# Scatter rows of a mixture-of-experts block: made on GpSimd between two scatters, two blocks ahead, as a sum in place of a maximum

## The chip, the cores and the metric

The kernel runs on one core of a Trainium2 chip. The metric is the device time of one execution in microseconds; before the change the median of three runs is 561.6 us (561.57 to 562.12). A core has a matrix engine (TensorE, PE in the profile), VectorE (DVE), ScalarE (ACT), GpSimd (POOL) and SyncE (SP), which only issues transfers. Each engine runs its own instructions in order, and they wait for one another through semaphores. Transfers (DMAs) are issued by SyncE, ScalarE and GpSimd; the scatters here are issued by GpSimd[...].

## What is computed

One transformer layer on 8 sequences of 512 tokens with 128 features, all in float32:

```
x = layernorm(x + attention(x))          # 16 heads, causal
probs = softmax(x @ gate_w.T)            # 14 experts
top2_p, top2_i = top_k(probs, 2)
w = top2_p / max(top2_p.sum(-1), 1e-10)
hh = gelu(x @ w1[e] + b1[e])             # 128 -> 256, for each expert e
all_out = hh @ w2[e] + b2[e]             # 256 -> 128
moe_out = w[:, 0] * all_out[top2_i[:, 0]] + w[:, 1] * all_out[top2_i[:, 1]]
x = layernorm(x + clip(x + moe_out, -100, 100))
```

Each token goes to the two experts with the highest probabilities, so there are 2 x 4096 = 8192 pairs of a token and an expert.

## The kernel before

The attention part works through the sequences in an order written out by hand (`jobs`, `at`). For each sequence `route` picks the two experts of every token, and GpSimd scatters the tokens' rows into a buffer `XS` in HBM, sorted by expert (`scatter("XS", ...)`, L793). A row has 130 numbers: 128 features, the weight of this expert (column `D`), and the row of the output buffer `OS` that the result belongs to (column `D + 1`, a whole number in float32).

The expert part then goes over `NBLK` = 45 blocks of `BT` = 256 rows of `XS`, each of one expert. The first `EARLY` = 11 blocks are full ones, planned from the first six sequences. The other 34 can have rows behind an expert's last token; for these `beyond` is 1,000,000 in the rows that hold no token and 0 in the others, so that their target lies outside `OS` and the scatter leaves them out (`bounds_check` = 8191). An iteration of the loop over the blocks (L1142) gives out, in this order:

- `load(i + 4)`: SyncE loads the block's rows into `xb`, one of six buffers (`into`).
- `begin(i + 2)`: ScalarE copies the expert's weights (`weights`), and `turn` has TensorE transpose the rows (L1048) and VectorE copy them out of PSUM into `xT` (L1050, named `bxT` in the profile). `turn` also makes the block's target rows on VectorE: for late blocks the maximum of column `D + 1` and `beyond` (L1054, `bto`), and for all blocks the cast to int32 (L1058, `bto_i`).
- `expert_in(i + 1)`: the first matmuls (L1066, `h`) and ScalarE's gelu (L1071, `hT`).
- `expert_out(i)`: the second matmuls (L1082, `o`); then for each half `s` of 128 rows VectorE multiplies by the weight (L1090, `ob`, eight buffers), and GpSimd scatters the half into `OS` by `bto_i` (L233).
- after every fourth block from block 12 on, `biases` of one sequence: a transpose (L1101, `wp`), a copy on VectorE (L1107, `wT`), a matmul (L1109, `bp`), and an addition on VectorE (L1112).

The routing of the last sequence (`last_route`, with its eight scatters into `XS`) and the plan of the late blocks are given out in pieces among the first blocks; dummy rows behind every expert's last token are written by SyncE and ScalarE (`fill`, L804 and L807). The first late block's load waits for all scatters into `XS`. When all scatters into `OS` have landed, the tail gathers the two results of each token, adds them and normalises.

Of the kernel before, what the change touches and what calls it, by code (L numbers as in the profile page):

```python
# [10 lines left out]
ALU = mybir.AluOpType  # L11
# [25 lines left out]
def kernel(  # L37
# [18 lines left out]
    nc = tc.nc  # L56
    B, T, D = x.shape
    E, _, F = w1.shape
# [9 lines left out]
    NBLK = (2 * N + E * (BT - 1)) // BT  # L68


    EARLY = -(-(2 * (B - 2) * T - E * (BT - 1)) // BT)
# [160 lines left out]
    def scatter(key, dst, idx, src, bound):  # L232
        inst = nc.gpsimd.indirect_dma_start(  # L233
            dst,
            bass.IndirectOffsetOnAxis(ap=idx, axis=0),
            src,
            None,
            bounds_check=bound,
            oob_is_err=False,
        )  # L240
        tc.declare_no_dep(inst.ins, group=key, reason="no two of them write the same row")
        tc.add_to_no_dep_group(key, inst.ins)
        scatters.setdefault(key, []).append(inst.ins)
        return inst
# [18 lines left out]
    with tc.tile_pool(name="work", bufs=2) as work, tc.tile_pool(  # L263
# [9 lines left out]
        def bank(name, dt=FP):  # L273
            return ps_m.tile([P, 2048 // mybir.dt.size(dt)], dt, tag="bank", name=name)
# [4 lines left out]
        wt = bank("wt")  # L279
# [317 lines left out]
        def divide(u):  # L597
            b, g = divmod(u, NG)
            oT = outs.pop(u)
            tr = bank(f"tr_{u}")  # L600
            for qb in range(NQ):
                nc.tensor.transpose(
                    tr[:, qb * P : (qb + 1) * P], oT[:, qb * P : (qb + 1) * P], ident
                )
            tr_v = tr.rearrange("p (q j s) -> p q j s", j=GH, s=HS)
            rec = work.tile([P, NQ, GH, 1], FP, tag="rec", name=f"rec_{u}")
            nc.vector.reciprocal(rec, tr_v[:, :, :, HD : HD + 1])
            if g == 0:
                attns[b] = work.tile(
                    [P, NQ, NG, GH, HD], FP, tag="attn", name=f"attn_{b}", bufs=1  # L610
                )
            nc.vector.tensor_tensor(
                attns[b][:, :, g],
                tr_v[:, :, :, 0:HD],
                rec.to_broadcast([P, NQ, GH, HD]),
                ALU.mult,
            )

        def project(b):

            attn = attns.pop(b)
            tp = bank(f"at_{b}")
            for qb in range(NQ):
                nc.tensor.transpose(
                    tp[:, qb * P : (qb + 1) * P],
                    attn[:, qb].rearrange("p g j d -> p (g j d)"),
                    ident,
                )
            aT = work.tile([P, T], FP, tag="aT", name=f"aT_{b}", bufs=1)
            nc.scalar.copy(aT, tp)  # L630
            outs["a", b] = aT, outs.pop(("x", b))
# [261 lines left out]
        beyond = plan.tile([P, SB, P], FP, tag="beyond", name="beyond")  # L893
# [85 lines left out]
                    at(r + 2, statistics, b, (2, 3))  # L979
                    at(r + 3, proceed, r + 3, route(b), 1)  # L980

        blocks = {}

        def load(i):
            where = wheres[i >= EARLY]
# [28 lines left out]
        s = -2  # L1014
# [20 lines left out]
        def weights(i):  # L1035
            n = i if i < EARLY else i - EARLY
            at_w = nc.scalar.value_load(
                wheres[i >= EARLY][0:1, 1, n : n + 1], min_val=0, max_val=(E - 1) * WW
            )
            wt = ffn.tile([P, WW], FP, tag="wt", name=f"wt_{i}", bufs=4)  # L1040
            nc.scalar.copy(wt, WR[:, bass.ds(at_w, WW)])  # L1041
            blocks[i].insert(1, wt)

        def turn(i):
            xb = blocks[i][0]
            tp = ps_x.tile([P, BT], FP, tag="x", name=f"x_{i}")
            for s in range(SB):
                nc.tensor.transpose(tp[:, s * P : (s + 1) * P], xb[:, s, 0:D], ident)  # L1048
            xT = ffn.tile([P, BT], FP, tag="xT", name=f"bxT_{i}")
            nc.vector.tensor_copy(xT, tp)  # L1050
            to = xb[:, :, D + 1]
            if i >= EARLY:
                to = ffn.tile([P, SB], FP, tag="to", name=f"bto_{i}")
                nc.vector.tensor_tensor(  # L1054
                    to, xb[:, :, D + 1], beyond[:, :, i - EARLY], ALU.max
                )
            to_i = ffn.tile([P, SB], I32, tag="to_i", name=f"bto_i_{i}", bufs=NBLK)
            nc.vector.tensor_copy(to_i, to)  # L1058
            blocks[i] += [xT, to_i]

        def expert_in(i):
            xb, wt, xT, to_i = blocks[i]
            hp = ps_h.tile([P, NFC, BT], FP, tag="h", name=f"h_{i}")
            hT = ffn.tile([P, NFC, BT], FP, tag="hT", name=f"hT_{i}")
            for f in range(NFC):
                nc.tensor.matmul(  # L1066
                    hp[:, f, :], wt[:, f * P : (f + 1) * P], xT, start=True, stop=True
                )
            for f in range(NFC):
                c = F + NFC * D + f  # L1070
                nc.scalar.activation(  # L1071
                    hT[:, f, :], hp[:, f, :], AF.Gelu, bias=wt[:, c : c + 1]
                )
            blocks[i].append(hT)

        def expert_out(i):
            xb, wt, xT, to_i, hT = blocks.pop(i)
            op = ps_o.tile([P, SB, D], FP, tag="o", name=f"o_{i}")
            ob = ffn.tile([P, SB, D], FP, tag="ob", name=f"ob_{i}", bufs=8)
            for s in range(SB):  # L1080
                for f in range(NFC):
                    nc.tensor.matmul(  # L1082
                        op[:, s, :],
                        hT[:, f, s * P : (s + 1) * P],
                        wt[:, F + f * D : F + (f + 1) * D],
                        start=(f == 0),
                        stop=(f == NFC - 1),
                    )
            for s in range(SB):
                nc.vector.tensor_scalar(  # L1090
                    ob[:, s, :], op[:, s, :], xb[:, s, D : D + 1], 0.0, ALU.mult, ALU.add
                )
                scatter("OS", OS[:, :], to_i[:, s : s + 1], ob[:, s, :], 2 * N - 1)


        acc = z_sb = x_sb
# [22 lines left out]
        def begin(i):  # L1119
            weights(i)  # L1120
            turn(i)
# [11 lines left out]
                fill(place_i, e)  # L1133

        begin(0)
        divide(u)
        begin(1)
        project(b)
        expert_in(0)
        residual(b)  # L1140
        statistics(b, range(NQ))
        for i in range(NBLK):  # L1142
            if i + AHEAD < NBLK:
                load(i + AHEAD)
            if i < 3:
                go_on(1)
            if i == 3:
                place_i = fill_place()
                late = plan_late()
                fills(range(0, 4))  # L1150
                go_on(4)
            if i == 4:
                fills(range(4, 8))
                go_on(4)
            if i + 2 < NBLK:
                begin(i + 2)
            if i < 3:
                go_on(1)
            if 3 <= i < 6:
                next(late, None)  # L1160
            if i + 1 < NBLK:
                expert_in(i + 1)
            if i < 3:
                go_on(1)
            if i == 5:
                fills(range(8, E))
            if 3 <= i < 7:
                next(late, None)
            expert_out(i)
            if i >= 12 and i % 4 == 0 and (i - 12) // 4 < B:  # L1170
                biases((i - 12) // 4)
# [100 lines left out]
```

## Time and profile before

| What | us |
|---|---|
| median of the runs (3) | 561.6 |
| the profiled execution, whole | 598.87 |
| its span, first to last instruction | 597.2 |
| first scatter into `OS` starts, us from the span's start | 394.21 |
| last scatter into `OS` starts | 555.52 |
| GpSimd: busy, share of the span | 337.2 (56%) |
| VectorE: busy, share of the span | 390.7 (65%) |
| TensorE: busy, share of the span | 477.9 (80%) |
| mean granted clock of TensorE | 0.911 of full |

The profile is of one execution, and every time of an instruction is from it; it took longer than the runs that were only timed. In a row of the profile `out<-in` names what is written and read, `L1090` is a line of the kernel, and a busy time is followed by the mean of one instruction in nanoseconds. An idle time is that of the engine just before the instruction; the name behind it is the work whose end the profile holds to have ended the wait. "issue" is time in which the engine waited for nothing that the profile shows. `SPq` and `POOLq` are the sequencers of SyncE and GpSimd, which set registers and issue transfers.

### The profile page before, as it was taken

The page shows a single profiled execution, that of the slowest core. Times are in us where ns is not written, and L with a number is a line of the kernel's source. Part 1 is how long each engine was busy: PE and PEld are TensorE (multiplying, and loading weights), DVE is VectorE, ACT ScalarE, POOL GpSimd, SP SyncE. Part 2 cuts the span into 40 slices and gives each one's busy share as a digit, 9 for nine tenths or more (in the row PEclk, how much of TensorE's full clock was granted, in tenths as well). Part 3 has the DMA queues.
Part 4 walks back from the last instruction along what each step waited for, and adds up shares of the span by engine and source line. Part 5 has one row for each costly group of instructions (what it writes and reads, how often), then busy time and mean ns, then how long its engine had stood idle before and what let it go on. Part 6 is the DMA issues. An engine that isn't in the chain of part 4 may idle for free. (4 is left out here: it accounts for less than half of the span.)

```text
span 597.2 us, 10892 instructions
## 1 busy us (share of the span) xinstructions
PE 477.9 (80%) x3371; PEld 294.5 (49%) x3371; DVE 390.7 (65%) x928; ACT 301.8 (51%) x476; POOL 337.2 (56%) x698
## 2 busy tenths in 40 slices
PE   1557999999999999998999887764688687887391
PEld 1233645455455554554554433453576576676140
DVE  4248687789888998998989868164234344433194
ACT  0203577677667766776665655462243343433044
POOL 5001434444875867848758885757455546666243
PEclk9866899999999999999999987788688889888697
DMA  6153324525444455344443552424332222230663
GB/s 170 58 158 101 95 70 159 146 88 148 147 142 131 135 153 154 127 148 151 133 134 112 173 157 63 104 57 131 110 101 71 67 60 59 79 85 5 161 175 88
DMA packets 69956, 68.75 MB, mean 115 GB/s; under 512 B 11644, under 2 KB 57829, under 8 KB 69898
## 3 DMA queue, kind: packets, MB, share of 16 engines
q1 hardware_dynamic: 58336, 56.03, 31.8%
q0 software_dynamic: 4928, 8.48, 4.4%
q10 hardware_dynamic: 6634, 3.55, 2.2%
q8 instruction: 27, 0.44, 0.3%
q14 instruction: 31, 0.25, 0.1%
HBM read 39.17 MB, written 27.98 MB: 112 GB/s over the span
## 5 line engine op out<-in xcount | busy, mean ns | idle before, releaser
L527 ACT ACTIVATE pt<-b 128x1024 f32<-128x1024 f32 x160 | 162.5, 1022 | 49.5 <-PE b L492 39.9
L503 POOL TENSOR_SCALAR_AFFINE_SELECT pt<-pt 128x256 f32<-128x256 f32 (+1 forms) x224 | 97.4, 451 | 88.1 <-ACT pt L527 87.1
L409 PE MATMUL f<-ring 72*128 72x384 bf16 (+3 forms) x512 | 114.5, 307 | 20.8 <-DMA ring<-qsc 9.5
L233 POOL DMA_INDIRECT OS<-ob,bto_i x90 | 88.4, 982 | 61.5 <-DVE ob L1090 40.8
L492 PE MATMUL b<-ring 75*128 75x384 bf16 (+3 forms) x512 | 99.3, 309 | 7.1 <-ACT pt L527 3.1
L549 PE MATMUL av<-pt,v_aug 128*32 128x512 f32 (+3 forms) x1024 | 85.8, 449 | 5.4 <-POOL pt L503 5.4
L461 DVE TENSOR_REDUCE mx<-f 128x2 f32<-128x1024 f32 x64 | 77.8, 1221 | 17.7 <-PE f L419 15.5
L419 PE MATMUL f<-causal_bf,ident_bf 128*128 128x256 bf16 (+1 forms) x320 | 82.4, 258 | 0.0
L454 DVE TENSOR_REDUCE mx<-f 128x8 f32<-128x1024 f32 x64 | 77.1, 1214 | 3.8 <-PE f L419 3.5
L1071 ACT ACTIVATE hT<-h,wt 128x256 f32<-128x256 f32 x90 | 37.8, 471 | 80.6 <-PE h L1066 39.7
L409 PEld LDWEIGHTS <-ring 72*128 72x128 bf16 x512 | 50.8, 100 | 55.3 <-issue 31.7
L1090 DVE TENSOR_SCALAR ob<-o,bxb 128x128 f32<-128x128 f32 x90 | 27.4, 346 | 65.7 <-PE o L1082 22.9
L1066 PE MATMUL h<-bxT,wt 128*128 128x256 f32 x180 | 55.9, 440 | 10.7 <-ACT wt L1041 5.5
L492 PEld LDWEIGHTS <-ring 75*128 75x128 bf16 x512 | 42.3, 100 | 41.8 <-issue 27.2
L1082 PE MATMUL o<-wt,hT 128*128 128x128 f32 x360 | 56.3, 306 | 7.0 <-ACT hT L1071 6.7
L1082 PEld LDWEIGHTS o<-wt,hT 128*128 128x128 f32 x360 | 55.1, 219 | 13.8 <-ACT hT L1071 8.3
L549 PEld LDWEIGHTS av<-pt,v_aug 128*32 128x32 f32 x1024 | 27.2, 110 | 54.5 <-issue 38.8
L449 DVE TENSOR_REDUCE mx<-f 128x4 f32<-128x1024 f32 x32 | 39.1, 1222 | 15.4 <-PE f L419 11.2
L1066 PEld LDWEIGHTS h<-bxT,wt 128*128 128x128 f32 x180 | 36.1, 223 | 16.0 <-ACT wt L1041 6.2
L419 PEld LDWEIGHTS <-ident_bf 128*128 128x128 bf16 x320 | 31.8, 99 | 15.0 <-issue 2.4
L233 POOL DMA_INDIRECT XS<-second,to_i x32 | 33.5, 1047 | 8.6 <-issue 8.6
L233 POOL DMA_INDIRECT XS<-y_sb,to_i x32 | 33.0, 1032 | 7.7 <-issue 6.0
(196 smaller groups left out, 609.6 us busy)
## 6 DMA issues: line engine op xcount, KB each, us to landing
ring<-ksc SPq DMA_DIRECT2D x32, 288.0 KB
ring<-qsc SPq DMA_DIRECT2D x96, 96.0 KB
osc<-oT SPq DMA_DIRECT2D x28, 256.0 KB
bxb<-XS SPq DMA_DIRECT2D x45, 130.0 KB
ring<-in_L_ffn_w_dram SPq DMA_DIRECT2D x28, 128.0 KB
qsc<-qpc SPq DMA_DIRECT2D x24, 128.0 KB
ksc<-kpc SPq DMA_DIRECT2D x24, 128.0 KB
x_sb<-in_L_attn_x_dram SPq DMA_DIRECT2D x8, 256.0 KB
```

The lines of the kernel that those rows point to most:

```text
L233: inst = nc.gpsimd.indirect_dma_start(dst, bass.IndirectOffsetOnAxis(ap=idx, axis=0), src, None, bounds_check=bound, oob_is_err=False,)
L409: nc.tensor.matmul(ps[:, col : col + W], qr[u % RING][0:KR, j, qb * P : (qb + 1) * P], kr[u % RING][0:KR, j, :W], start=first, stop=False, ...
L419: nc.tensor.matmul(out, ident_bf, causal_bf[:, 0:n, :], start=False, stop=True, skip_group_check=True,)
L449: nc.vector.reduce_max(mx[:, :, 5], ps.rearrange("p b (s k) -> p (b s) k", s=2), axis=AX.X)
L454: nc.vector.reduce_max(mx[:, j : j + 2, 1:5], ps.rearrange("p b (s k) -> p b s k", k=P), axis=AX.X,)
L461: nc.vector.reduce_max(mx[:, j : j + 2, 7], ps, axis=AX.X)
L492: nc.tensor.matmul(ps[:, col : col + W], kr[u % RING][:, j, kb * P : (kb + 1) * P], qr[u % RING][:, j, kb * P :], start=first, stop=True, ...
L503: nc.gpsimd.affine_select(out=view, in_=view, pattern=[[0, k] for k in n] + [[1, P]], compare_op=ALU.is_ge, fill=0.0, base=0, channel_mult ...
L527: nc.scalar.activation(pt, ps, AF.Exp, scale=SCALE)
L549: nc.tensor.matmul(avs[u][HS * j : HS * (j + 1), kb * P :], v_aug[b % 2][:, kb, g * GH + j, :], p, start=(kb == 0), stop=(kb == 2),)
L1066: nc.tensor.matmul(hp[:, f, :], wt[:, f * P : (f + 1) * P], xT, start=True, stop=True)
L1082: nc.tensor.matmul(op[:, s, :], hT[:, f, s * P : (s + 1) * P], wt[:, F + f * D : F + (f + 1) * D], start=(f == 0), stop=(f == NFC - 1),)
```

## The change

The making of the target rows leaves `turn` for a function of its own, `rows_of`. It runs on GpSimd in place of VectorE, takes the sum of the column and `beyond` in place of their maximum (a row behind the last token is still out of bounds), and is given out between the two scatters of `expert_out`, for the block two ahead; for blocks 0 and 1 it is given out after their `begin`. The dictionary `rows_to` carries the result from there to the scatters of its own block.

```diff
-        blocks = {}
+        blocks, rows_to = {}, {}
...
             nc.vector.tensor_copy(xT, tp)
+            blocks[i].append(xT)
+
+        def rows_of(i):
+            xb = blocks[i][0]
             to = xb[:, :, D + 1]
             if i >= EARLY:
                 to = ffn.tile([P, SB], FP, tag="to", name=f"bto_{i}")
-                nc.vector.tensor_tensor(
-                    to, xb[:, :, D + 1], beyond[:, :, i - EARLY], ALU.max
+                nc.gpsimd.tensor_tensor(
+                    to, xb[:, :, D + 1], beyond[:, :, i - EARLY], ALU.add
                 )
             to_i = ffn.tile([P, SB], I32, tag="to_i", name=f"bto_i_{i}", bufs=NBLK)
-            nc.vector.tensor_copy(to_i, to)
-            blocks[i] += [xT, to_i]
+            nc.gpsimd.tensor_copy(to_i, to)
+            rows_to[i] = to_i
...
         def expert_out(i):
-            xb, wt, xT, to_i, hT = blocks.pop(i)
+            xb, wt, xT, hT = blocks.pop(i)
+            to_i = rows_to.pop(i)
...
                 scatter("OS", OS[:, :], to_i[:, s : s + 1], ob[:, s, :], 2 * N - 1)
+                if s == 0 and i + 2 < NBLK:
+                    rows_of(i + 2)
...
         begin(0)
+        rows_of(0)
         divide(u)
         begin(1)
+        rows_of(1)
```

More of the change, by code (lines that the diff above doesn't have):

```diff
@@ L1053, in turn @@
                 to = ffn.tile([P, SB], FP, tag="to", name=f"bto_{i}")
-                nc.vector.tensor_tensor(
-                    to, xb[:, :, D + 1], beyond[:, :, i - EARLY], ALU.max
+                nc.gpsimd.tensor_tensor(
+                    to, xb[:, :, D + 1], beyond[:, :, i - EARLY], ALU.add
                 )
             to_i = ffn.tile([P, SB], I32, tag="to_i", name=f"bto_i_{i}", bufs=NBLK)
-            nc.vector.tensor_copy(to_i, to)
-            blocks[i] += [xT, to_i]
+            nc.gpsimd.tensor_copy(to_i, to)
+            rows_to[i] = to_i
         def expert_in(i):
-            xb, wt, xT, to_i = blocks[i]
+            _, wt, xT = blocks[i]
             hp = ps_h.tile([P, NFC, BT], FP, tag="h", name=f"h_{i}")
```

## The prediction

> **What bounds the kernel now.** I read the page's engine and group rows first, to find the stage that the change touches and its costliest engine; then GpSimd's timeline, for the rhythm of the scatters; then the timelines of VectorE and TensorE beside it and the chain of work that ended last, to see what GpSimd waits for. The page:
>
> ```profile
> PE 477.9 (80%) x3371; PEld 294.5 (49%) x3371; DVE 390.7 (65%) x928; ACT 301.8 (51%) x476; POOL 337.2 (56%) x698
> L233 POOL DMA_INDIRECT OS<-ob,bto_i x90 | 88.4, 982 | 61.5 <-DVE ob L1090 40.8
> ```
>
> The second row is a group (busy us, mean ns | idle us before it, and what ended most of that): 90 scatters of expert outputs, two for each of 45 blocks, 0.98 us each, and before 25 of them 40.8 us of waiting for `ob`. Averaged over the span GpSimd is 56% busy and TensorE 80%, but the change lies in the expert stage alone, so the rhythm there decides. GpSimd's timeline at two places, the first blocks and the end of the stage (start, duration, engine, line, and the idle time before it with its releaser):
>
> ```profile
> 393.11 0.20 POOL L220 TENSOR_TENSOR shift<-stats,rstd 128x4 f32<-128x4 f32 x1
> 393.40 0.19 POOL L221 TENSOR_SCALAR shift<-shift 128x4 f32<-128x4 f32 x1
> ...
> 395.61 0.97 POOL L233 DMA_INDIRECT OS<-ob,bto_i  x1 [0.30 <-DVE best L732]
> 396.57 0.21 POOL L737 COPY second<-ids 128x4 f32<-128x4 f32 x1
> ...
> 397.28 0.20 POOL L742 TENSOR_TENSOR gap<-gap,rstd 128x4 f32<-128x4 f32 x1
> 398.04 1.01 POOL L233 DMA_INDIRECT OS<-ob,bto_i  x1 [0.56 <-issue]
> ...
> 546.52 0.98 POOL L233 DMA_INDIRECT OS<-ob,bto_i  x1 [1.98 <-DVE ob L1090]
> 547.81 0.98 POOL L233 DMA_INDIRECT OS<-ob,bto_i  x1 [0.31 <-issue]
> ...
> 554.23 0.98 POOL L233 DMA_INDIRECT OS<-ob,bto_i  x1 [0.30 <-issue]
> 555.52 0.98 POOL L233 DMA_INDIRECT OS<-ob,bto_i  x1 [0.30 <-issue]
> ```
>
> With nothing to wait for, a scatter starts 1.29 us after the one before it (554.23 to 555.52): 2.57 us a block. From 394.21, where block 0's first scatter starts, to 556.50 GpSimd runs the 90 scatters and the last sequence's 8 (rows into `XS`). That is 98 x 1.285 = 125.9 us, and some 3.3 us of small operations between them: 129.2 us of the 162.3 us. The other 33.1 us are idle, which fits the page: 40.8 us less the ordinary 0.30 us before each of 25 scatters is 33.3.
>
> So the question is whether that idle time is there when nobody profiles. The profiled execution took 598.87 us (span 597.2 and 1.67 around it), the median of the runs is 561.6: 37.3 us less. Outside the stage the span has 394.2 us ahead and 40.7 us behind; if those take as long unprofiled, 561.6 - 1.67 - 434.9 = 125.0 us are left for a stage in which GpSimd has 129.2 us of work. Almost all of GpSimd's waiting has to be gone in the runs, and some 4 us elsewhere too. The waits also look like delays that the work itself doesn't make. VectorE's timeline, then TensorE's, then the chain of work that ended last:
>
> ```profile
> 535.68 0.17 DVE L1058 CAST bto_i<-bto 128x2 int32<-128x2 f32 x1
> 539.08 0.61 DVE L1090 TENSOR_SCALAR ob<-o,bxb 128x128 f32<-128x128 f32 x2 [3.23 <-PE wp L1101]
> ```
> ```profile
> 535.52 1.05 PE L1082 MATMUL o<-wt,hT 128*128 128x128 f32 x8
> ```
> ```profile
> 412.67 0.69 SPq L804
> 413.36 0.70 issue
> ...
> 423.31 0.15 SPq L804
> ```
>
> `ob` at 539.08 has its operands from the matmuls that end at 536.57, and starts 2.5 us late; in 411 to 422 SyncE's register steps take 0.7 us each, where the same line takes 0.15 us at 423. I take it that the profiled execution hears of finished work late while scatters run back to back, and that unprofiled **GpSimd's scatter queue sets the pace of the expert stage** with few waits. TensorE is not far behind it: 1.97 us a block at full clock and 1.5 us for the biases of every fourth, 2.35 us a block, more at the granted 0.83 to 0.9 of these windows.
>
> **The change, part by part.** *Removed from VectorE:* the maximum (34 blocks) and the cast (45).
>
> ```profile
> L1054 DVE TENSOR_TENSOR bto<-bxb,beyond x34: 150/152/154, 436.9 to 546.8; 128x2 f32<-128x2 f32 x34
> L1058 DVE CAST bto_i<-bto x34: 169/170/219, 437.1 to 546.9; 128x2 int32<-128x2 f32 x34
> ```
>
> In the chain they stand between `bxT` and the next `ob` with 0.22 us together, some ten times in the stage, before the biases' matmul above all: 2.2 us on the path where TensorE sets the pace, nothing where GpSimd does.
>
> *Added to GpSimd:* the rows of blocks 0 and 1 are two casts ahead of the stage, in the 3.68 us that GpSimd idles up to 391.69: nothing (without that cover 2 x 0.29 = 0.6 us). The other 43 come between the two scatters of block i-2. Cost of one, from the rows above: an operation starts 0.98 us after a scatter's start (396.57 after 395.61, no gap), the second of two dependent ones 0.29 us after the first (393.11 to 393.40), and a scatter 0.76 us after a short operation's start (397.28 to 398.04: the issue gap is 0.56 us there, not 0.30). So late blocks (sum and cast) have 0.98 + 0.29 + 0.76 = 2.03 us from scatter to scatter where they had 1.29, **+0.74 us**; early ones (cast alone) 1.74, +0.45. Sum: 34 x 0.74 + 9 x 0.45 = 25.2 + 4.1 = **29.2 us on GpSimd's queue**.
>
> The 128x2 forms aren't in GpSimd's trace. Lower end: the two 0.20 us alone, the issue hidden behind them: 34 x 0.40 + 9 x 0.20 = 15.4 us. Upper end: 0.81 us from operation to scatter (393.40 to 394.21) and the first scatter after an operation at its longest 1.09: +0.90 and +0.61, 36 us. The rule that speaks against the change is in the Trainium skill, GPSIMD Engine Reference, section Engine selection: two-input elementwise work on GpSimd runs about twice as slow as on VectorE. Twice the 0.152 us row is 0.30 us for the sum, where GpSimd's own 128x4 row has 0.20; by the rule 34 x 0.10 more, 32.6 us. The row is nearer (same engine, as short), so I keep 29.2. The sum in place of the maximum costs nothing by either: one two-input pass.
>
> *Waits added:* the row operation waits for block i+2's load, and behind it on GpSimd stand the block's second scatter and all later ones. The transposes of block i+2 are ahead of block i's matmuls in TensorE's order and need the same load, so it landed before block i's first scatter could start: nothing. Loads now wait for the row operation that read their buffer; six buffers let GpSimd lag some four blocks (about 13 us) before a load is late, and when it is, GpSimd itself has scatters left for those blocks. In the last sequence's routing four casts come ahead of its last `XS` scatters, 4 x 0.45 = 1.8 us later, and with them the first late load; GpSimd has blocks 4 to 10 to scatter meanwhile. Both are in the sum already.
>
> *The end:* blocks 41 to 44 scatter back to back from 546.52 even in the profile, and two of them now carry row operations: 2 x 0.74 = 1.5 us that no wait absorbs.
>
> **The sum.** 29.2 us less what GpSimd still waits in the unprofiled stage, which the longer queue absorbs. By the balance above that is what the rest of the program runs faster unprofiled, less 4 us; TensorE is busy nearly throughout from 60 to 380 us, so I allow 4 to 12 us there and take 3 us of remaining waits. 561.6 + 29.2 - 3 = **588 us**. In the profile itself part of the 29.2 would go into the 33.1 us of waits, so its span should rise by less.
>
> **The rivals.** *A, the forecast: GpSimd paces, few waits are left.* For it: the balance of 125.0 against 129.2 us. 576 to 597 from the ends 15.4 and 36.
>
> *B: TensorE and VectorE share the pace.* If scatters issue faster when unprofiled, or the rest shrinks by 20 us, some 15 us of waits are left: 561.6 + 29.2 - 15 = 576 (567 to 582). For it: TensorE's 2.35 us at full clock is nearly GpSimd's 2.57 and exceeds it when throttled. Against it: the attention part has no 20 us to give.
>
> *C: hidden.* Waits of over 29 us stay, the end's 1.5 us and VectorE's 2.2 cancel: 561. This is also the case in which the change does not do anything. Against it: the 37.3 us would have to come from elsewhere.
>
> *D, the other side: the breaks between scatters pay.* Waits of the kind at 539.08 end about 1.9 us after the start of the last scatter in a row. A pair of operations between scatters leaves at most two in a row, and between 394 and 404, where such operations stand now, SyncE's steps keep their 0.03 to 0.3 us. If a good part of the 33.1 us were real unprofiled, breaking the rows could return it; faster from the point where it returns more than the 29.2 us put in: at best -4 us, 557. Against it: the unprofiled runs leave no room for such waits.
>
> **How the numbers follow.** A 0.66, B 0.18, C 0.07, D 0.09. About 0.2% (1.1 us) is what a measurement of this kernel tells from no change. Faster is D and a little of C, 0.10; same most of C, 0.05; slower A, B and the rest, 0.85. The range leaves out C, D and A's top: 567 to 596.
>
> **What would show it.** In the changed profile: the two row operations on GpSimd at about 0.2 us each, 34 and 45 times; starts in a block about 2.0 us apart and 1.29 to the next block; fewer long idle times before scatters, GpSimd's busy share in the stage up; `ob` to `bxT` to `ob` 0.3 us shorter on VectorE; the last scatter ending at least 1.5 us after the last `ob` than it does now. It would be wrong if the medians differ by less than 5 us (GpSimd had room, B or C), or if an operation between scatters costs other than 0.74 us, or if the row operations wait for loads, which I put at nothing.

## The result and the profile after

| | us |
|---|---|
| before, median of 6 runs | 561.51 (559.6 to 562.12) |
| after, median of 6 runs | 591.45 (588.84 to 593.77) |
| ratio after to before, 95% interval | 1.0528 (1.0498 to 1.0559) |
| forecast | 588.0 (567 to 596) |

The change costs 29.9 us. The profiled execution of the changed kernel is one of the six: 589.98 us, span 588.3.

One thing has to be known to read the rest: the kernel before took some 600 us on three chips (23, 39 and 33 timed runs) and some 560 us on a fourth (23 and 7 runs), so every ratio below is of runs on one chip, and "600-us chip" and "560-us chip" say which kind it was. The comparison above has the time of the second kind. The profile of before that the prediction read (598.87 us) has the time and the waits of the first. Which chips these two were is not on record, and no chip was measured again much later, so it is likely, and not shown, that the chip decides and not the hour.

A ratio and its interval are estimated from each kernel's runs within 1.5% of its fastest, and are not the quotient of the medians beside them, which are over all its runs.

The engine row, GpSimd's scatter group and the two new groups in the stage of the changed kernel (busy us, mean ns | idle us before it and what ended it):

```profile
PE 467.8 (80%) x3371; PEld 287.8 (49%) x3371; DVE 382.3 (65%) x849; ACT 302.5 (51%) x476; POOL 351.8 (60%) x777
...
L233 POOL DMA_INDIRECT OS<-ob,bto_i x90 | 88.6, 984 | 39.3 <-issue 22.6
```
```profile
L1058 POOL TENSOR_TENSOR bto<-bxb,beyond 128x2 f32<-128x2 f32 x34 | 7.3, 215 | 0.5
L1062 POOL CAST bto_i<-bto 128x2 int32<-128x2 f32 x34 | 6.3, 184 | 2.2
...
L1062 POOL CAST bto_i<-bxb 128x2 int32<-128x2 f32 x9 | 1.9, 208 | 0.0
```

The 79 operations have moved from VectorE (928 to 849) to GpSimd (698 to 777). Before the scatters, "issue" has become the main idle time (22.6 us). GpSimd's timeline, early blocks and then late ones, shows where it sits:

```profile
421.34 0.97 POOL L233 DMA_INDIRECT OS<-ob,bto_i  x1 [0.31 <-DVE bxT L1050]
422.31 0.20 POOL L1062 CAST bto_i<-bxb 128x2 int32<-128x2 f32 x1
422.67 0.98 POOL L233 DMA_INDIRECT OS<-ob,bto_i  x1 [0.16 <-DVE ob L1095]
423.96 0.97 POOL L233 DMA_INDIRECT OS<-ob,bto_i  x1 [0.30 <-issue]
...
539.55 0.97 POOL L233 DMA_INDIRECT OS<-ob,bto_i  x1 [0.30 <-issue]
540.54 0.21 POOL L1058 TENSOR_TENSOR bto<-bxb,beyond 128x2 f32<-128x2 f32 x1
540.82 0.18 POOL L1062 CAST bto_i<-bto 128x2 int32<-128x2 f32 x1
541.60 0.99 POOL L233 DMA_INDIRECT OS<-ob,bto_i  x1 [0.60 <-issue]
542.89 0.98 POOL L233 DMA_INDIRECT OS<-ob,bto_i  x1 [0.30 <-issue]
```

With the lone cast of an early block the two scatters start 1.33 us apart (421.34 to 422.67): some 0.05 us more than the ordinary 1.285, because 0.20 us of cast is followed by a gap of only 0.16 us. With the dependent pair of a late block they start 2.05 us apart (539.55 to 541.60): after the cast GpSimd is idle for 0.60 us before the next scatter runs. The two operations take 0.4 us of the 0.76 us that this adds; the rest comes where the second operation waits for the first, which leaves an idle gap of 0.60 us before the scatter in place of 0.16 (the experiments below take the two apart).

In 158.3 us from the first scatter into `OS` to the end of the last, GpSimd has one idle time longer than 0.65 us:

```profile
478.04 0.18 POOL L1062 CAST bto_i<-bto 128x2 int32<-128x2 f32 x1
481.40 1.00 POOL L233 DMA_INDIRECT OS<-ob,bto_i  x1 [3.18 <-DVE bxT L1050]
```

The releaser that the row names, `bxT`, is hardly the cause: in other profiles the same stop carries another name. GpSimd's sequencer issues nothing between 478.1 and 481.2. Five of the profiles below have a stop of 3.18 us before the same scatter, the 50th into `OS`, on 600-us chips; all have pairs of operations on GpSimd. One more has 2.18 us there, on the 560-us chip. No transfer of instructions was under way during the stop in the changed kernel's profile (the nearest start at 469.8 and 487.9 us). What it is stays open.

### The profile page after: what moved, and what is told of

Its sections match the earlier page's. It is cut to its first block, busy times and chain, and to the rows that moved or that the text cites. A ratio compares the mean times of both kernels' runs of the same rounds, so it can differ in the third digit from the quotient of the medians.

```text
span 588.3 us, 11005 instructions
## 1 busy us (share of the span) xinstructions
PE 467.8 (80%) x3371; PEld 287.8 (49%) x3371; DVE 382.3 (65%) x849; ACT 302.5 (51%) x476; POOL 351.8 (60%) x777
## 4 chain that ended last, share of the span: by engine, by line
PE 43%; DVE 15%; DMA 13%; POOL 10%; ACT 9%; issue 7%; ACTq 2%; SPq 1%; POOLq 0%; DVEq 0%
PE av L549 9%; PE f L409 8%; PE b L492 6%; ACT pt L527 6%; POOL OS L233 5%; PE h L1070 4%; PE o L1087 4%; DMA bxb<-XS 3%; PE f L419 3%; DMA recT<-rd 2%; DMA rd<-den 2%; ACT oT L559 2%; DVE bn L210 2%; POOL pt L503 2%; PE q L358 2%
## 5 line engine op out<-in xcount | busy, mean ns | idle before, releaser
L409 PE MATMUL f<-ring 72*128 72x384 bf16 (+3 forms) x512 | 116.8, 312 | 17.4 <-DMA ring<-qsc 8.5
L233 POOL DMA_INDIRECT OS<-ob,bto_i x90 | 88.6, 984 | 39.3 <-issue 22.6
L419 PE MATMUL f<-causal_bf,ident_bf 128*128 128x256 bf16 (+1 forms) x320 | 83.6, 261 | 0.0
L409 PEld LDWEIGHTS <-ring 72*128 72x128 bf16 x512 | 51.4, 102 | 52.7 <-issue 29.4
L1070 PE MATMUL h<-bxT,wt 128*128 128x256 f32 x180 | 51.1, 410 | 7.7 <-ACT wt L1041 7.0
L1087 PEld LDWEIGHTS o<-wt,hT 128*128 128x128 f32 x360 | 50.6, 203 | 3.3 <-ACT hT L1075 0.3
L1087 PE MATMUL o<-wt,hT 128*128 128x128 f32 x360 | 50.8, 288 | 0.0
L1070 PEld LDWEIGHTS h<-bxT,wt 128*128 128x128 f32 x180 | 33.7, 209 | 11.6 <-ACT wt L1041 7.7
```

Source lines behind the costliest of these rows:

```text
L233: inst = nc.gpsimd.indirect_dma_start(dst, bass.IndirectOffsetOnAxis(ap=idx, axis=0), src, None, bounds_check=bound, oob_is_err=False,)
L409: nc.tensor.matmul(ps[:, col : col + W], qr[u % RING][0:KR, j, qb * P : (qb + 1) * P], kr[u % RING][0:KR, j, :W], start=first, stop=False, ...
L419: nc.tensor.matmul(out, ident_bf, causal_bf[:, 0:n, :], start=False, stop=True, skip_group_check=True,)
L1070: nc.tensor.matmul(hp[:, f, :], wt[:, f * P : (f + 1) * P], xT, start=True, stop=True)
L1087: nc.tensor.matmul(op[:, s, :], hT[:, f, s * P : (s + 1) * P], wt[:, F + f * D : F + (f + 1) * D], start=(f == 0), stop=(f == NFC - 1),)
```

## The experiments

For every profile the table splits the stage (from the start of the first scatter into `OS` to the end of the last, from GpSimd's timeline) in two: long waits, which are idle times of GpSimd above 0.65 us, each less the ordinary 0.30; and the rest, GpSimd's queue itself. It is the summary of what follows. A profile is of one execution, up to 5.5 us from the median of its kernel's runs, so differences of a few us in the waits say nothing.

| kernel | chip | stage us | long waits (number) | the rest |
|---|---|---|---|---|
| before, the profile of the prediction | 600 | 162.3 | 33.4 (19) | 128.9 |
| before again | 600 | 163.2 | 34.3 (20) | 128.9 |
| before again | 560 | 129.0 | 0 | 129.0 |
| the change | 560 | 158.3 | 2.9 (1) | 155.5 |
| the change again | 600 | 163.8 | 8.1 (4) | 155.6 |
| row operations behind both scatters | 560 | 158.4 | 3.1 (3) | 155.3 |
| cast alone on GpSimd | 560 | 131.0 | 0 | 131.0 |
| unused pair on GpSimd | 600 | 165.4 | 10.0 (4) | 155.4 |
| unused pair, every second block | 600 | 161.8 | 19.5 (10) | 142.4 |
| two more copies in the pair | 600 | 180.9 | 8.1 (4) | 172.8 |
| sum a block earlier | 600 | 177.9 | 40.4 (18) | 137.5 |
| one whole-number operation | 600 | 181.0 | 48.2 (18) | 132.8 |
| the same, and a dependent cast | 600 | 164.6 | 9.5 (4) | 155.2 |
| whole-number rows on VectorE | 600 | 155.5 | 26.4 (19) | 129.1 |

**Before, unchanged.**

> The kernel before, profiled once more, to see whether the profiled execution's 598.87 us and GpSimd's 33 us of waits come back. Theory (GpSimd's queue paces the unprofiled runs, and the waits belong to that profiled execution): another profile either shows them again, near 598 us, while the timed runs stay at 561.5, or, if its execution is one like the timed runs, spans some 560 us with under 5 us of waits before the scatters and a scatter every 1.29 us from the first block to the last. Rival (TensorE and VectorE pace): a profile near 560 us has 10 us or more of GpSimd's waits for ob in it.

Measured: 600.82 us profiled, beside 601.63 us median of 23 runs that were only timed. So on this chip the timed runs have the profile's time: profiling does not cost 37 us. The waits of the prediction's profile come with the executions of 600 us, profiled or not, and the prediction's reason for setting them aside (that profiling makes them) is wrong, although setting them aside was right for the comparison that it forecast.

**The change, unchanged, on such a chip.**

> The changed kernel again, beside runs of the kernel before on the same chip. In the last comparison the kernel before took 601.6 us in 23 runs, 40 us more than in the first one, and its profile had GpSimd's waits of 1.5 to 3.6 us between rows of scatters in it; the changed kernel's profile, at 590.0 us, has one wait. Theory 1 (a chip or hour either has these waits or not, and the first comparison was made without them, for both): where the kernel before takes 561, the changed one takes 590; where it takes 601, the changed one takes 600 to 610, as the unused pair did (606), and its profile has GpSimd's waits at the first late loads in it. Theory 2 (breaking the rows of scatters takes the waits away wherever they are): 588 to 594 us beside 601 or beside 561 alike, so the sign of the change hangs on the chip.

Measured: 603.24 us (20 runs) beside 599.97, ratio 1.0063 (1.0033 to 1.0094). The same edit that costs 5.3% on a 560-us chip costs 0.6% here, within the first theory's range and outside the second's. The table says why: GpSimd's queue grows by the same 26.7 us (128.9 to 155.6), and 26.2 us of long waits vanish (34.3 to 8.1).

**An unused pair of the same operations on GpSimd, rows still made on VectorE.**

```diff
+        def rows_unused(i):
+            to = ids[:, :, 0]
+            if i >= EARLY:
+                to = ffn.tile([P, SB], FP, tag="un", name=f"un_{i}")
+                nc.gpsimd.tensor_tensor(to, ids[:, :, 0], beyond[:, :, i - EARLY], ALU.add)
+            un_i = ffn.tile([P, SB], I32, tag="un_i", name=f"un_i_{i}", bufs=NBLK)
+            nc.gpsimd.tensor_copy(un_i, to)
...
                 scatter("OS", OS[:, :], to_i[:, s : s + 1], ob[:, s, :], 2 * N - 1)
+                if s == 0 and i + 2 < NBLK:
+                    rows_unused(i + 2)
```

> The kernel before, with the rows still made on VectorE; only the pair of operations (a sum for late blocks and a cast that waits for it) is added on GpSimd between a block's two scatters, on a constant in place of the block's rows, and nobody uses what it makes. No load and no scatter waits for it. Theory (time in GpSimd's queue is the whole cause): as slow as the changed kernel, 589 to 594 us. Rival 1 (the new waits of loads for the row operation, or of it for loads, cost part): several us under the changed kernel, 575 to 586. Rival 2 (VectorE's relief gains something that the change kept): several us over it, 595 or more.

Measured: 606.33 us (20 runs) beside 601.63, ratio 1.0074 (1.0048 to 1.01), which overlaps the change's own 1.0063. The ranges expected were for a 560-us chip, so only the ratios can be compared. Adding the operations to GpSimd without taking any from VectorE and without any wait for a load does what the change does, on chips of this kind. VectorE's relief, the new dependences and the loads that now wait for GpSimd are together worth no more than the some 2 us that the intervals leave. On a 560-us chip this kernel was not run.

**The sum made one block earlier**, so that no operation in a gap depends on the one just ahead of it.

```diff
+        def sum_of(i):
+            if EARLY <= i < NBLK:
+                to = ffn.tile([P, SB], FP, tag="to", name=f"bto_{i}")
+                nc.gpsimd.tensor_tensor(
+                    to, blocks[i][0][:, :, D + 1], beyond[:, :, i - EARLY], ALU.add
+                )
+                sums_of[i] = to
...
-                nc.gpsimd.tensor_tensor(
-                    to, xb[:, :, D + 1], beyond[:, :, i - EARLY], ALU.add
-                )
+                to = sums_of.pop(i)
...
                     rows_of(i + 2)
+                if s == 0:
+                    sum_of(i + 3)
```

> The changed kernel, with the sum of a late block made one block earlier: between a block's two scatters GpSimd first casts the sum made in the block before, then makes the next block's sum, so that no operation waits for the one just ahead of it. Same operations, same number. The changed profile has 0.36 us from a lone cast to the next scatter's start, but 0.28 and then 0.78 us where the cast waits for the sum. Theory (it is the wait of one GpSimd operation for the other that keeps the sequencer from preparing the scatter): two unbound operations take 0.98 + 0.2 + 0.4 = 1.6 us from scatter to scatter in place of 2.05, so 34 x 0.45 = 15 us come back: 576 us. Rival (each GpSimd operation costs its own 0.37 us, bound or not): 589 to 593 us.

Measured: 615.24 us (4 runs) beside 601.63, ratio 1.0197 (1.012 to 1.0274). The expected 576 us was for a 560-us chip, so the 39 us between them are mostly the chip's. The miss is in the sign: it was to be 15 us faster than the change, and its ratio is 1.0197 where the change has 1.0063. It taught most. GpSimd's timeline of this kernel:

```profile
511.62 0.20 POOL L1069 CAST bto_i<-bto 128x2 int32<-128x2 f32 x1
511.76 0.20 POOL L1058 TENSOR_TENSOR bto<-bxb,beyond 128x2 f32<-128x2 f32 x1
512.12 0.99 POOL L233 DMA_INDIRECT OS<-ob,bto_i  x1 [0.16 <-issue]
516.34 0.97 POOL L233 DMA_INDIRECT OS<-ob,bto_i  x1 [3.22 <-DVE ob L1102]
517.31 0.20 POOL L1069 CAST bto_i<-bto 128x2 int32<-128x2 f32 x1
517.45 0.21 POOL L1058 TENSOR_TENSOR bto<-bxb,beyond 128x2 f32<-128x2 f32 x1
517.83 0.99 POOL L233 DMA_INDIRECT OS<-ob,bto_i  x1 [0.17 <-issue]
```

The step it was built for works: the gap before the scatter is 0.16 us where the change has 0.60, and the scatters around a pair start 1.49 us apart (516.34 to 517.83) where the change has 2.05. So of the 0.76 us that a dependent pair adds, some 0.2 are the operations and some 0.56 the dependence. On a 560-us chip, where this kernel was not run, that makes an estimate of 34 x 0.2 + 9 x 0.05 = some 7 us for the whole move. But 3.22 us are then lost waiting for `ob`, and so on through the stage: 40.4 us of long waits where the change has 8.1 on such a chip. A cheaper queue gave a slower kernel.

**Rows in int32, one operation on GpSimd.** `XS` carries the row as int32 bits and `beyond` is copied to int32 once, so that the sum alone gives the row.

```diff
-                nc.gpsimd.tensor_tensor(
-                    to, xb[:, :, D + 1], beyond[:, :, i - EARLY], ALU.add
-                )
...
-            nc.gpsimd.tensor_copy(to_i, to)
+            if i >= EARLY:
+                nc.gpsimd.tensor_tensor(to_i, row_i, beyond_i[:, i - EARLY, :], ALU.add)
+            else:
+                nc.gpsimd.tensor_copy(to_i, row_i)
```

> The changed kernel, with the target rows kept as int32 from the start (column 129 holds the bits of an integer, the bound is added as an integer): one GpSimd operation between the two scatters for every block, none that waits for another. Theory: 0.98 + 0.36 = 1.34 us from scatter to scatter as for the early blocks, 0.05 us over two bare scatters: 43 x 0.05 = 2 us, 562 to 566 us. Rival (moving the rows to GpSimd costs as such, by the waits between loads, rows and scatters): 575 us or more.

Measured: 625.34 us (613.67 to 627.09, 4 runs, no interval) beside 601.63; the lowest of the four is above the highest run of before (605.01). The profile is of a run of 623.77 us. A miss of the same kind: the operation costs little in the queue (132.8 us beside 128.9), and the waits rise to 48.2 us. The two misses together brought the next theory: on 600-us chips a wait for `ob` comes when GpSimd is handed scatter after scatter without a stop of its sequencer, and the dependent pair is such a stop.

**Rows in int32 on VectorE, one operation, nothing on GpSimd.** The edit is shown against the kernel before.

```diff
-                nc.vector.tensor_tensor(
-                    to, xb[:, :, D + 1], beyond[:, :, i - EARLY], ALU.max
-                )
...
-            nc.vector.tensor_copy(to_i, to)
+            if i >= EARLY:
+                nc.vector.tensor_tensor(to_i, row_i, beyond_i[:, i - EARLY, :], ALU.add)
+            else:
+                nc.vector.tensor_copy(to_i, row_i)
```

> The target rows kept as int32 from the start and made on VectorE behind the copy of the transposed rows, as before the change: one operation there in place of two (late) or a cast (early), nothing new on GpSimd. Theory (GpSimd's scatter queue paces the stage): VectorE's 0.2 us a block less change nothing: within 3 us of the kernel before beside it, 561 or 601. Rival (TensorE behind VectorE paces): 2 to 7 us under it.

Measured: 597.53 us (20 runs) beside 599.97, ratio 0.998 (0.9949 to 1.0012). Taking 34 operations from VectorE is worth nothing that can be told from zero. It also clears the int32 rows as such of blame for the 625 us of the experiment ahead.

**The one whole-number operation, and a cast that depends on it.**

```diff
                 nc.gpsimd.tensor_tensor(to_i, row_i, beyond_i[:, i - EARLY, :], ALU.add)
+                un_i = ffn.tile([P, SB], I32, tag="un_i", name=f"un_i_{i}", bufs=NBLK)
+                nc.gpsimd.tensor_copy(un_i, to_i)
```

> The kernel with whole-number rows and one GpSimd operation (625 beside 602 for the kernel before) gets, in its 34 late blocks, a cast of the row into a tile that nobody reads: the cast depends on the operation ahead of it, so GpSimd's sequencer stops before it and the next scatter's issue gap goes from 0.16 back to 0.60 us. Theory 1 (waits for ob come where GpSimd is handed scatter after scatter without such a stop, and a stop lets the news of finished work through): although GpSimd gets more work, the waits shrink and the time falls to the change's own, 600 to 606 beside a before of 600. Theory 2 (the waits come from something else in that kernel, its whole-number operands or its loads): it stays at 615 to 640, with waits of 2 to 4 us before scatters all through the stage.

Measured: 602.63 us (14 runs) beside 599.14, ratio 1.0084 (1.0057 to 1.0111). More work on GpSimd, and 3.5 us above before where the kernel without the cast was 12 to 25 us above it. Its timeline has a gap of 0.59 us, and scatters that wait for nothing:

```profile
527.08 0.97 POOL L234 DMA_INDIRECT OS<-ob,bto_i  x1 [0.30 <-issue]
528.07 0.20 POOL L1061 TENSOR_TENSOR bto_i<-bxb,beyond_i 128x2 int32<-128x2 int32 x1
528.34 0.18 POOL L1063 COPY un_i<-bto_i 128x2 int32<-128x2 int32 x1
529.12 0.99 POOL L234 DMA_INDIRECT OS<-ob,bto_i  x1 [0.59 <-issue]
530.42 0.98 POOL L234 DMA_INDIRECT OS<-ob,bto_i  x1 [0.30 <-DVE ob L1098]
```

Long waits fall from 48.2 to 9.5 us. The edit touches nothing but GpSimd's rhythm, so on these chips the waits hang on the rhythm.

**Two more dependent copies in each late pair.**

```diff
+                for k in range(2):
+                    more = ffn.tile([P, SB], FP, tag=f"more{k}", name=f"bto{k}_{i}")
+                    nc.gpsimd.tensor_copy(more, to)
+                    to = more
```

> The change with two more dependent copies on GpSimd between the sum and the cast of the 34 late blocks: 0.28 us each, so 34 x 0.56 = 19 us more in GpSimd's queue. Theory 1 (with the change GpSimd's queue sets the pace without waits, so every further us there is paid in full): 19 us above the change, 1.03 times it, 620 to 624 where the change has 603. Theory 2 (on these chips TensorE at its lower granted clock sets the pace and GpSimd has room, which is why the change costs only 0.6% there): 603 to 610, the waits for ob that the change still has get shorter.

Measured: 619.56 us (4 runs) beside 599.14, ratio 1.0322 (1.0255 to 1.0389). The queue grows by another 17.2 us (155.6 to 172.8), the waits stay at 8.1, and the ratio goes from 1.0063 to 1.0322, which is 15.5 us of 600. So with the stop in place GpSimd's queue sets the pace on these chips too, and further work there is paid nearly in full. TensorE at a lower clock, with room left on GpSimd, would have hidden it.

**The unused pair in every second block only.**

```diff
-                if s == 0 and i + 2 < NBLK:
+                if s == 0 and i % 2 == 0 and i + 2 < NBLK:
                     rows_unused(i + 2)
```

> The kernel before with the unused dependent pair on GpSimd in every second block only (rows still made on VectorE), so 4 scatters in a row and then a stop, where the pair in every block cost 1.0074 of before. Cost in the queue: half of the 26 us, 13 us. Theory 1 (stops of GpSimd's sequencer do away with waits for ob; they come after three or more scatters in a row): about half to all of the 30 us of waits go, so 585 to 600 beside 600, below the pair in every block. Theory 2 (stops do nothing; the queue has room because TensorE paces): 600 to 604, between before and the pair in every block.

Measured: 598.23 us (20 runs) beside 599.14, ratio 0.9942 (0.9912 to 0.9972). Half the stops cost half (13.5 us of queue) and take away nearly half of the waits (34.3 to 19.5). The ratio says 0.6% faster than before. But the medians over all runs differ by 0.15% only, so that it beats before is not shown. It wasn't run on a 560-us chip, where before has no long waits to take away.

**Before, once more, and the cast alone on GpSimd.** This set fell on a 560-us chip.

> The kernel before, looked at once more, on another chip if one is given. If this chip is like those of the last three sets: 600, waits for ob of 1.5 to 4.5 us before scatters through the whole stage (some 34 us), and some 25 register steps of SyncE of 0.6 to 0.8 us while the scatters run. If it is like the one on which the kernel before took 561.5: 561, fewer than 5 us of such waits after the first scatter, and next to no such steps.

Measured: 559.68 us for the profiled execution, beside a median of 561.22. This is the profile that the prediction lacked, its scatter group and the end of GpSimd's timeline:

```profile
L233 POOL DMA_INDIRECT OS<-ob,bto_i x90 | 88.4, 982 | 28.1 <-issue 8.2
```
```profile
388.48 1.09 POOL L233 DMA_INDIRECT OS<-ob,bto_i  x1 [0.51 <-DVE ob L1090]
...
515.22 0.98 POOL L233 DMA_INDIRECT OS<-ob,bto_i  x1 [0.30 <-issue]
516.50 0.98 POOL L233 DMA_INDIRECT OS<-ob,bto_i  x1 [0.30 <-issue]
```

The stage runs from 388.48 to 517.48: 129.0 us, all of it GpSimd's queue and no long wait. The expectation held for SyncE's register steps as well. Of all its sequencer's steps in the stage, 22 take 0.6 to 0.8 us here, but none of them sets a register: 21 are semaphore steps of the loads (L991). In before on the 600-us chip 25 are as long, and 14 of them load, set or check registers. One line's register steps on SyncE, first there and then here (shortest, median and longest in ns):

```profile
L804 SPq FUSED_REGOPS  x7: 16/152/712, 404.0 to 426.5; - x7
```
```profile
L804 SPq FUSED_REGOPS  x7: 152/152/156, 397.1 to 407.0; - x7
```

Such a row names no tile of another engine that the step could wait for. So on the 600-us chip more is late than the news of finished work.

The timelines of the other engines differ too. Here, with scatters back to back, `ob` starts 0.04 us after the matmuls of `o` end (471.10 + 1.05 = 472.15), and ScalarE's `hT` 0.10 us after those of `h` (470.23 + 1.03 = 471.26):

```profile
470.23 1.03 PE L1066 MATMUL h<-bxT,wt 128*128 128x256 f32 x4
471.10 1.05 PE L1082 MATMUL o<-wt,hT 128*128 128x128 f32 x8
471.36 0.84 ACT L1071 ACTIVATE hT<-h,wt 128x256 f32<-128x256 f32 x2 [0.62 <-PE h L1066]
471.52 0.98 POOL L233 DMA_INDIRECT OS<-ob,bto_i  x1 [0.30 <-DVE bto_i L1058]
472.19 0.61 DVE L1090 TENSOR_SCALAR ob<-o,bxb 128x128 f32<-128x128 f32 x2 [0.76 <-PE o L1082]
472.81 0.98 POOL L233 DMA_INDIRECT OS<-ob,bto_i  x1 [0.30 <-DVE ob L1090]
```

And on the 600-us chip (before, unchanged), `o` ends at 538.78, just as fast, and `ob` starts 2.46 us later, 1.89 us after the start of the last scatter of a row. ScalarE is late as well: `hT` starts 1.23 us after its matmuls end (536.86 + 1.03 = 537.89). So the delay is not one of `ob` or its buffers alone.

```profile
536.86 1.03 PE L1066 MATMUL h<-bxT,wt 128*128 128x256 f32 x4
...
537.73 1.05 PE L1082 MATMUL o<-wt,hT 128*128 128x128 f32 x8
538.06 0.98 POOL L233 DMA_INDIRECT OS<-ob,bto_i  x1 [0.30 <-issue]
...
539.12 0.84 ACT L1071 ACTIVATE hT<-h,wt 128x256 f32<-128x256 f32 x2 [1.76 <-PE x L1048]
539.35 0.98 POOL L233 DMA_INDIRECT OS<-ob,bto_i  x1 [0.30 <-issue]
...
541.24 0.61 DVE L1090 TENSOR_SCALAR ob<-o,bxb 128x128 f32<-128x128 f32 x2 [3.19 <-PE wp L1101]
...
541.87 0.98 POOL L233 DMA_INDIRECT OS<-ob,bto_i  x1 [1.54 <-DVE ob L1090]
```

The other half of this set moves the cast alone:

```diff
-
-        def rows_of(i):
-            xb = blocks[i][0]
             to = xb[:, :, D + 1]
             if i >= EARLY:
-                to = ffn.tile([P, SB], FP, tag="to", name=f"bto_{i}")
-                nc.gpsimd.tensor_tensor(
+                to = ffn.tile([P, SB], FP, tag="to", name=f"bto_{i}", bufs=NBLK)
+                nc.vector.tensor_tensor(
                     to, xb[:, :, D + 1], beyond[:, :, i - EARLY], ALU.add
                 )
+            sums[i] = to
+
+        def rows_of(i):
+            to = sums.pop(i)
...
```

> Half of the move: the sum stays on VectorE (as a sum), the cast alone is made by GpSimd between the two scatters, in all blocks. No operation there depends on one just ahead of it. What was measured of the change's early blocks says 1.33 us from scatter to scatter, 0.05 more than without the cast: 43 x 0.05 = 2 us in GpSimd's queue. Theory 1 (the cost is the stop of the sequencer ahead of the second dependent operation, and the same stop does away with waits on the chips where back-to-back scatters hold up the others): on a chip where before takes 561, 562 to 565; on one where it takes 600, no stop and so waits as before or more, 600 to 620. Theory 2 (the cost is GpSimd's time for the operations, 0.2 us and more for each): on a chip where before takes 561, 570 to 577.

Measured: 563.30 us (20 runs) beside 561.22, ratio 1.0026 (1.0001 to 1.005). Its timeline on the 560-us chip:

```profile
425.75 0.97 POOL L233 DMA_INDIRECT OS<-ob,bto_i  x1 [0.30 <-DVE ob L1096]
426.72 0.21 POOL L1063 CAST bto_i<-bto 128x2 int32<-128x2 f32 x1
427.09 0.98 POOL L233 DMA_INDIRECT OS<-ob,bto_i  x1 [0.16 <-issue]
428.37 0.97 POOL L233 DMA_INDIRECT OS<-ob,bto_i  x1 [0.30 <-DVE bto L1055]
```

43 casts of 0.21 us on the engine that sets the pace, and the stage grows by 2.0 us (129.0 to 131.0), as 43 x 0.05 says. If operations were paid by their own time it would be 9 us. What is paid for in the change is the second operation, and most of all its dependence on the first. VectorE makes the sum here in 0.152 us, as it made the maximum before (0.152), so the sum in place of the maximum costs nothing.

**The row operations behind both scatters.**

```diff
-                if s == 0 and i + 2 < NBLK:
+                if s == 1 and i + 2 < NBLK:
                     rows_of(i + 2)
```

> The change with the row operations of block i+2 behind both scatters of block i instead of between them: the same operations, the same count, another place. Theory 1 (what counts is GpSimd's queue time, 0.75 us for each dependent pair, wherever it stands between two scatters, and that there is a stop in every block): as the change, 589 to 594 where before takes 561, 600 to 606 where it takes 600. Theory 2 (the place matters, since the block's second scatter stands behind the row operations): more than 3 us below the change on either kind of chip.

Measured, on a 560-us chip: 591.36 us (4 runs) beside 561.07, ratio 1.0548 (1.0471 to 1.0625); its stage is the change's (158.4 us), and its long waits come to as much (3.1 us, three of them, 2.18 us the longest). Whether the pair stands between the two scatters or behind them makes no difference that these runs show.

## Why the prediction was right, point by point

**What bounds the kernel: right.** Its balance left 125.0 us for a stage in which GpSimd has 129.2 us of work; the 560-us profile of before has 129.0 us and no long wait. The 4 us between the two are in the stretch ahead of the stage, which is 5.7 us shorter there than in the prediction's profile (388.48 against 394.21). **The reason given for the missing waits: wrong.** It held profiling to be their cause. Timed runs on 600-us chips take as long as the profile that has them, and a profile on a 560-us chip has none.

**Late blocks, +0.74 us: right**, 0.75 to 0.76 measured. (The rows that it cites have 0.96 us from a scatter's start to an operation's, not 0.98; the changed kernel has 0.99.) The row it came from, an operation to a scatter with a 0.56 us gap, was a dependent operation, as the cast is.

**Early blocks, +0.45 us: wrong.** It measured +0.05, in the change and in the cast alone. The term of 9 x 0.45 = 4.1 us is 0.5 us. The step took the 0.76 us from operation to scatter from a row in which the operation depends on the one ahead (`gap` from `gap`), and put it on a cast that depends on nothing just ahead of it.

**The sum in the queue, 29.2 us: 26.5 measured** (129.0 to 155.5), and 34 x 0.75 + 9 x 0.05 = 26.0.

**Less 3 us of remaining waits: wrong**, there were none to absorb anything. **Missing from the sum:** the one stop of 3.18 us that the changed kernel has and before has not, 2.9 us beyond the ordinary gap. So 26.5 + 2.9 = 29.4 us of stage, and the runs differ by 29.9; the forecast of +26.4 came as close as it did partly by luck: an early term 3.6 us too large and a stop of 2.9 us not foreseen nearly cancel, and the 3 us taken off remain as the error. The spread of 576 to 597 for this forecast does not follow from its ends either: 561.6 + 15.4 - 3 and 561.6 + 36 - 3 are 574 and 595. The measured 591.5 lies in both.

**The rule that spoke against the change** (the Trainium skill, GPSIMD Engine Reference, section Engine selection: about twice VectorE's time) was weighed against GpSimd's own 0.20 us row, and the row was right: the sum takes 0.215 us where VectorE takes 0.152 for the maximum and for the sum, 1.4 times. By the rule it would have been 0.30.

**Costed at nothing.** Waits of the row operation for its load: right, GpSimd has no long wait but the stop. Rows of blocks 0 and 1: right; on the 560-us chip where before's first scatter starts at 388.48, that of the kernel with the row operations behind both scatters, which has these rows too, starts at 388.38. VectorE's relief: nothing measurable in the unused pair and the whole-number rows, both on 600-us chips; on a 560-us chip the cast alone takes 45 operations from VectorE and costs the 2 us of the queue. The sum in place of the maximum: right, 0.152 us each on VectorE.

**The rivals.** B and C, room left on GpSimd: out for 560-us chips by the profile of before there. D, that breaks between scatters pay: on 560-us chips there is nothing to win. On 600-us chips its mechanism is real and it falls short: the change takes back 26.2 us of waits and puts in 26.7 us of queue, and the runs say +0.6%. The prediction dismissed it for want of room in the timed runs; that held for the chip of the comparison alone.

**Left open.** Why on three chips finished work is heard of late while scatters run back to back, SyncE's register steps are late as well, and on the fourth neither happens, is not known from these runs. (That it is the chips, and not the hour, is itself not shown.) TensorE's granted clock is lower there (before, from the stage's start to 430 us and from 430 to 470: 0.78 and 0.88 against 0.96 and 1.00), but a late `ob` behind an `o` that ran at full speed, and waits that come and go with GpSimd's rhythm alone, speak against the clock as the cause.

## What to carry to other kernels

Before moving small operations to an engine that issues scatters, ask whether that engine's queue sets the pace, and whether one operation depends on the one just ahead of it: here 43 lone casts cost 2 us and 34 dependent pairs some 26, where pairs without the dependence would cost some 7 by the estimate above. When a profiled time and the timed runs differ by several per cent, have both kinds of execution in hand before reading waits off the profile; they may come from different chips. This change costs 5% on one kind and 0.6% on the other, so it is to be judged on both.

## What the runs showed of the hardware that was not expected

- One operation on GpSimd between two scatters is nearly free if it depends on nothing just ahead: the issue gap shrinks from 0.30 to 0.16 us and the scatters start 1.33 us apart in place of 1.29. Two that do not depend on one another make it 1.49 us. If the second depends on the first, the gap is 0.60 us and the scatters start 2.05 us apart.
- The same kernel took 560 us on one chip and 600 us on three others. The difference is 33 to 34 us of waits in one stage and some 6 us ahead of it. In rows of back-to-back scatters VectorE can start some 2.5 us after TensorE has finished its operands on the 600-us chips, and starts 0.04 us after on the other. Register steps of SyncE that take 0.15 us there take up to 0.7 us on the 600-us chips.
- On the chips that wait, a stop of GpSimd's sequencer of 0.6 us once in a block takes away four fifths of the waits (48.2 to 9.5 us), and making the queue cheaper without it makes the kernel slower (615 us, and 614 to 627 us, beside 602).
- With pairs of operations added to it, GpSimd's sequencer stands still for 3.18 us before one scatter, the 50th into `OS`, the same to the hundredth in six profiles on both kinds of chip, with nothing in the trace that it waits for. Its cause is open.
